# TensorE repeats a product of the identity in four places where it waits

## The chip, the cores and the metric

The kernel runs on one core of a Trainium2 chip. The core has a matrix engine (TensorE; its matmuls are PE in the profile, its weight loads PEld), a vector engine (VectorE, DVE), a scalar engine (ScalarE, ACT), GpSimd (POOL) and SyncE (SP), which issues most of the DMAs. Each engine works through its own instructions in the order in which the program gives them, and engines wait for one another through semaphores. The metric is the device time of one execution, in microseconds; lower is better.

## The reference

Sixteen images of 128 channels and 32 x 32 points, all in float32, pass through two layers. Each layer has two halves, and each half adds its result to its input:

```python
x = x + _L0_conv_ref(_ln_c(x), ...)      # attention, heads of 32, softmaxes over q and k
t = _to_tokens(x)
t = t + _L0_ffn_ref(_ln_t(t), ...)       # causal spectral filters (FFT convolution) and 3 taps
x = _from_tokens(t, x)
x = x + _L1_conv_ref(_ln_c(x), ...)      # conv 3x3, scale and shift, relu, conv 3x3, relu
t = _to_tokens(x)
t = t + _L1_ffn_ref(_ln_t(t), ...)       # 64 experts, each pools its 8 best tokens of an image
```

The last half in short: a gate gives each of the 1024 tokens of an image a logit for each of 64 experts; softmax over the tokens; each expert takes its eight largest, sums those tokens with the gate's weights, passes the sum through a hidden layer of 512 with a gelu, and adds its output back to the same tokens with the same weights.

## The kernel before

One program holds everything, with the queues' order fixed by hand or by a planner; the engines do not reorder it, and so a line of Python that stands earlier runs earlier on its engine. Lines are those of the profile of the kernel before.

The begin. `ident` (128 x 128) is built first. Sixteen samples of attention are laid out in the list `period`: each pass of the loop over `p` emits every name in the list once, for the sample `p + d`. Names that matter here are `tokens` (L152 transposes of an image into the PSUM tile `big`), `filters` (a generator that prepares the spectral filters; its first products are L644, from `wf` and `phi`), `group` (L390, the image's statistic), `norm` (L144 on ACT, eight slabs of 128 tokens), `channels` (L162 transposes back), `k` (L439) and `q_` (L421). A PSUM ring named `s` with two slots holds small tiles. Two small products (L338, `pw`, read by DVE's copies at L339) have used both slots before the first pass.

The spectral stage follows (L790 generates filters, L814 multiplies spectra with them, ACT copies each result `py` out at L875). Its last outputs are combined by DVE, written to DRAM and read back as `y` by layer 1.

Layer 1. A planner (`planned`) gives each step of `table` for each of the 16 samples a place in one order, from costs and due times. For the first image, TensorE starts with `inverse` (L1074: for the even classes it reads `y` itself, then POOL's `z`, and for the odd classes DVE's `z`, L1020). Then come `tokens` (L152), the convolutions in a transformed domain (L958 in `products`, PSUM ring `cv` with three slots of 128 x 512), `last` (DVE, L1219, the end of the convolution's half), and for every second image the steps of a pair of images: `logits` (L1261), `largest`, `exp`, `replace`, `gates`, `turn` (L152 on the gates, copied by ACT at L1301), `pool` (L1308), `pooled` (L1321). `channels` (L162) of the second norm feeds `logits` through ACT's copy `tk` (L1253). The order that the planner makes is kept by the loop over `order`.

The experts. Weights come as 32 transfers of 1 MB (`load_half`, `we`) into a ring of nine buffers, which are those that layer 1 uses up to then; transfer h + 9 waits until buffer h has been read. Groups of four experts run through `hidden` (L1482 on the weights and L1489 on the bias, both in four column groups of 32), gelu on ACT (L1494), `turn` (L1502), `output` (L1513) and `collect` (L1524). DVE then weights the outputs (`ob`, L1554) from transposes in `pob` (L1550), and the last sums (L1572, `pfy`) multiply gates and `ob`; DVE, or ACT and POOL, add them to `x` and the images are written.

The first transfers of gates and weights wait for `tk` and `tt` buffers of layer 1; `gates` of the last pair stay in SBUF.

```python
getattr(samples[b], arg[0])(*(
    getattr(samples[b], a) if a in ("va", "vb") else a for a in arg[1:]
))
```

Here the loop over `order` emits one step of one sample.

## Time and profile before

| | |
|---|---|
| median of three runs | 1273.64 us (1272.99 to 1274.5) |
| the profiled execution's own time | 1271.01 us |
| its span, first to last instruction | 1269.2 us |
| mean granted TensorE clock | 0.967 |
| PE busy | 1149.1 us, 91% of the span |
| weight loads | 934.4 us, 74% |
| DVE busy | 936.2 us, 74% |
| ACT busy | 725.9 us, 57% |
| POOL busy | 605.3 us, 48% |
| DMA | 164.64 MB, 130 GB/s over the span |

The stages, by the lines that run: attention to about 402 us, the spectral stage to 661, layer 1's convolutions and gates to about 1159, the experts to 1240, the last sums and the writes to the end.

A page of the profile divides the span into 40 slices and gives for each the busy share of each engine in tenths, the clock that was granted to TensorE (PEclk, tenths of full speed) and the share of the DMA engines that was busy. A line of a group shows the source line, engine, operation, written tile and read tiles, their shapes, how often, busy time and the mean of one. Matmul records are pipelined; a record's duration is longer than the distance to the next one, so a sum over many is read from the first start to the last end. A float32 matmul stands as two records where it is a product, and as one where it is a transpose. In the rows of one line, durations in ns are shortest/median/longest. The chain of waits follows the work that ended last back from the last instruction.

### The profile page before, as it was taken

Reading aid. Unit: us, or ns where it says so; the run is one execution under the profiler, and the core shown is the slowest. Engines: PE = TensorE matmul, PEld = TensorE weight load, DVE = VectorE, ACT = ScalarE, POOL = GpSimd, SP = SyncE. Lnnn points to the kernel's source line nnn. Section 1 sums busy time; section 2 is a strip of 40 time slices with the busy share of each in tenths; the row PEclk is TensorE's granted clock in tenths of the full one; section 3 lists DMA queues with packets and bytes.
Section 4 is the critical chain, followed back from the end, with each engine's and each line's share of the span. In section 5 each row is a group of like instructions: output and inputs, shape, how many; then the busy total and the mean of one; then the engine's idle time right before and its main releaser. Section 6 shows DMA issues by size and latency. Waiting matters only on the chain. (4 is left out here: it accounts for less than half of the span.)

```text
span 1269.2 us, 34025 instructions
## 1 busy us (share of the span) xinstructions
PE 1149.1 (91%) x14244; PEld 934.4 (74%) x14244; DVE 936.2 (74%) x1944; ACT 725.9 (57%) x1420; POOL 605.3 (48%) x801
## 2 busy tenths in 40 slices
PE   4889999999997999999976999999999999977975
PEld 3677777777776998888865888888898888853432
DVE  5788888888765777776765798889898888772325
ACT  4777777767654777777742354565565556542111
POOL 2335545565666688888863444333353442210002
PEclk9999999999998999999998999999999999985998
DMA  7105343443345244444458231213222212055976
GB/s 264 33 30 165 117 139 124 134 158 111 106 134 183 87 136 137 137 136 136 130 196 244 72 81 34 83 34 84 67 55 77 70 50 101 27 190 190 389 285 265
DMA packets 88346, 164.64 MB, mean 130 GB/s; under 512 B 5632, under 2 KB 41728, under 8 KB 87552
## 3 DMA queue, kind: packets, MB, share of 16 engines
q1 hardware_dynamic: 87312, 159.05, 38.6%
q0 software_dynamic: 880, 3.41, 0.8%
q8 instruction: 112, 1.84, 0.6%
q14 instruction: 42, 0.34, 0.1%
HBM read 105.03 MB, written 57.41 MB: 128 GB/s over the span
## 5 line engine op out<-in xcount | busy, mean ns | idle before, releaser
L958 PE MATMUL pcv<-v,cw 128*128 128x256 f32 x1152 | 259.7, 381 | 0.7 <-POOL v L1144 0.7
L958 PEld LDWEIGHTS pcv<-v,cw 128*128 128x128 f32 x1152 | 215.9, 191 | 34.3 <-issue 4.9
L801 DVE COPY g<-pg 128x512 f32<-128x512 f32 x196 | 127.8, 682 | 77.1 <-PE pg L790 77.1
L803 ACT COPY g<-pg 128x512 f32<-128x512 f32 x316 | 161.2, 605 | 31.7 <-PE pg L790 30.9
L790 PE MATMUL pg<-ph,mst 32*128 32x128 f32 x4096 | 139.6, 278 | 5.0 <-issue 3.5
L790 PEld LDWEIGHTS pg<-ph,mst 32*128 32x128 f32 x4096 | 126.0, 186 | 19.1 <-issue 12.4
L814 PE MATMUL py<-g,v 128*32 128x128 f32 x4096 | 127.9, 276 | 8.5 <-POOL v L781 5.7
L814 PEld LDWEIGHTS py<-g,v 128*32 128x32 f32 x4096 | 110.1, 111 | 18.3 <-POOL v L781 5.8
L144 ACT ACTIVATE tok<-tok,sts 128x128 f32<-128x128 f32 x256 | 101.9, 480 | 16.8 <-DVE sts L1031 13.4
L135 DVE BATCH_NORM_STATS2 bst<-big 128x6 f32<-128x256 f32 x256 | 91.1, 416 | 23.3 <-PE big L152 14.1
L781 POOL TENSOR_TENSOR v<-xc 128x256 f32<-128x256 f32 x128 | 99.8, 803 | 8.9 <-DMA xd<-x 8.9
L626 PE MATMUL big<-u,mu 128*128 128x128 f32 (+4 forms) x384 | 86.0, 380 | 0.0
L1144 POOL TENSOR_TENSOR v<-abss 128x256 f32<-128x256 f32 x64 | 49.1, 788 | 66.1 <-DVE abss L1140 54.3
L277 POOL TENSOR_TENSOR xf<-ab 128x256 f32<-128x256 f32 x34 | 24.8, 729 | 112.3 <-DVE ab L244 112.3
L1163 POOL TENSOR_TENSOR yo<-abss 128x256 f32<-128x256 f32 x32 | 23.5, 736 | 109.1 <-DVE abss L1159 109.1
L626 PEld LDWEIGHTS big<-u,mu 128*128 128x128 f32 x384 | 56.7, 191 | 18.0 <-issue 15.4
L875 ACT COPY yt<-py 128x512 f32<-128x512 f32 x64 | 37.5, 586 | 48.9 <-PE py L814 26.4
L1580 POOL TENSOR_TENSOR x<-yt,x 128x1024 f32<-128x1024 f32 x4 | 9.4, 2359 | 115.2 <-ACT yt L1579 115.2
L559 PE MATMUL big<-wf,ub 128*128 128x256 f32 x256 | 62.0, 385 | 0.2
L144 ACT ACTIVATE tt<-tt,sts 128x128 f32<-128x128 f32 x128 | 51.1, 481 | 14.6 <-DVE sts L1031 14.6
L152 PEld LDWEIGHTS big<-ident,x 128*128 128x128 f32 x384 | 46.0, 146 | 17.7 <-issue 10.5
L782 POOL TENSOR_SCALAR v<-v 128x256 f32<-128x256 f32 x64 | 55.2, 862 | 5.6
(247 smaller groups left out, 2480.5 us busy)
## 6 DMA issues: line engine op xcount, KB each, us to landing
we<-in_weight SPq DMA_DIRECT2D x32, 1024.0 KB, 9.9
vd<-xf SPq DMA_DIRECT2D x16, 1024.0 KB, 5.1
xc<-vd SPq DMA_DIRECT2D x64, 256.0 KB, 3.2
yd<-ys SPq DMA_DIRECT2D x32, 512.0 KB, 4.0
y<-yd SPq DMA_DIRECT2D x14, 896.0 KB, 6.7
x<-in_x SPq DMA_DIRECT2D x16, 512.0 KB, 4.6
mi<-in_M_phi SPq DMA_DIRECT2D x16, 512.0 KB, 4.7
xd<-x SPq DMA_DIRECT2D x16, 512.0 KB, 6.1
```

The lines of the kernel that those rows point to most:

```text
L135: nc.vector.bn_stats(bst[:, j : j + 2, :].rearrange("p j s -> p (j s)"), src[:, j : j + 2, :].rearrange("p j c -> p c j"),)
L144: nc.scalar.activation(dst[:, j, :], src[:, j, :], AF.Identity, bias=nm[:, j : j + 1], scale=r[:, j : j + 1],)
L559: nc.tensor.matmul(dst, self.ub[:, q, :], wf[:, q, :], start=True, stop=True)
L626: nc.tensor.matmul(self.pa[:, a:hi], mu[:, NF - 1 - si, tap, :], self.u[:, a - tap : hi - tap], start=(tap == 0), stop=(tap == KU - 1),)
L781: nc.gpsimd.tensor_tensor(vv[:, x, 1:, bs], e, o, op)
L782: nc.gpsimd.tensor_scalar(v[:, :, 0, bs], v[:, :, 2, bs], -1.0, None, ALU.mult)
L790: nc.tensor.matmul(pg[r][:, i], mst[rs, 4 * q + i, :], ph[rs, c, :], start=True, stop=True,)
L801: nc.vector.tensor_copy(dst, src)
L803: nc.scalar.copy(dst, src)
L814: nc.tensor.matmul(py[rows, x, kl, :], v[:, (x * NM + m) * JL + jl, 1 - ri : 3 - ri, :] .rearrange("p k b -> p (k b)"), g[:, ((x * 2 + ri) ...
L958: nc.tensor.matmul(pc[:, i], wt[:, dy, k, :], v[:, k, dy * WT : dy * WT + HT], start=(dy == 0), stop=(dy == 2),)
L1144: nc.gpsimd.tensor_tensor(v[:, k, WT : WT + HT], self.ab[:, 0], self.ab[:, 1], op)
```

## The change

A function `keep` takes a pool, a ring's name and a count. It takes one tile `wm` from that ring and writes the product of the identity with two copies of itself into it, `count` times over, 128 x 256 float32. Nothing reads the tile. Calls stand at these places of TensorE's order:

- the begin: nine after `tokens` of image 1, eight after the first products of the filters, three after `channels` of image 0, three after `k` of image 1;
- ahead of layer 1: thirty-three ahead of the first `inverse`;
- the last pair's chain: four after `turn` of images 12 and 13, eight after their `pooled`, eleven after `logits` of images 14 and 15, one after their `turn`;
- ahead of the last sums: four after the transposes into `pob`.

Together that is 84 products. The instructions of the other engines stay as they were and in the same order.

```diff
+    def keep(ps, tag, count):
+
+        if count:
+            wm = ps.tile([P, 2, P], F32, name="wm", tag=tag, bufs={"s": 2, "cv": 3}[tag])
+        for _ in range(count):
+            nc.tensor.matmul(
+                wm, ident, ident.unsqueeze(1).to_broadcast([P, 2, P]), start=True, stop=True
+            )
...
+            idle = {("tokens", 1): 9, ("filters", 0): 8, ("channels", 0): 3, ("k", 1): 3}
...
                         if name == "filters":
                             next(setting, None)
+                            keep(ps, "s", idle.pop((name, 0), 0) if p > -reach else 0)
                         elif 0 <= b < B:
                             if name == "tokens":
                                 samples[b] = Attention(b)
                             getattr(samples[b], "q_" if name == "q" else name)()
+                            keep(ps, "s", idle.get((name, b), 0))
...
+        idle = {(13, "turn"): 4, (13, "pooled"): 8, (15, "logits"): 11, (15, "turn"): 1}
...
             samples = [None] * B
+            keep(ps, "cv", 33)
             for b, name in order:
...
                     getattr(samples[b], a) if a in ("va", "vb") else a for a in arg[1:]
                 ))
+                keep(ps, "cv", idle.get((b, name), 0))
...
                     pob[:, q, :], ot[:, 2 * q : 2 * q + 2, :].rearrange("p j e -> p (j e)"), ident
                 )
+            keep(ps, "cv", 4)
             for q in range(NPAIR):
```

## The prediction

> **What bounds the kernel now.** I read the page's slices first: TensorE (PE) is busy in nine tenths of nearly every slice, so a stage gains if TensorE has less to do or does it faster. The row of the granted clock says where it is not at full speed.

> ```profile
> PE   4889999999997999999976999999999999977975
> ...
> PEclk9999999999998999999998999999999999985998
> DMA  7105343443345244444458231213222212055976
> ```

> Each slice is 31.7 us. The dips are at the end (slices 36, 37 and 40) and in the middle (26); the first slice hides another. What a clock level does to an instruction is in the rows of single lines: shortest, median and longest record of the pooling products and of the hidden layer's.

> ```profile
> L1308 PE MATMUL pp<-tt,gtt x256: 272/273/473, 809.3 to 1157.3; 128*64 128x128 f32 x128
> L1482 PE MATMUL ph<-we,pooled x128: 592/617/1063, 1159.1 to 1230.4; 128*32 128x512 f32 x128
> ```

> ```profile
> 657.58:660.99 3.41, 0.00 (x0) 0.00 (x0) 1.58 (x5) 1.52 (x3) 0.01 (x1) 1.00 0.90 311
> 660.99:664.40 3.41, 0.00 (x0) 0.00 (x0) 2.75 (x6) 0.00 (x0) 0.00 (x0) 0.50 1.02 360
> ...
> 1125.20:1128.62 3.42, 1.11 (x20) 1.11 (x22) 3.21 (x8) 3.32 (x8) 0.73 (x1) 1.00 0.98 286
> 1128.62:1132.03 3.41, 3.41 (x25) 2.82 (x22) 3.38 (x3) 0.77 (x3) 0.00 (x0) 0.50 1.04 389
> 1132.03:1135.44 3.41, 1.14 (x10) 0.90 (x9) 1.67 (x6) 1.85 (x2) 0.20 (x1) 1.00 0.99 336
> ...
> 1145.68:1149.10 3.42, 0.00 (x0) 0.00 (x0) 2.57 (x5) 0.69 (x1) 0.00 (x0) 1.00 0.81 252
> 1149.10:1152.51 3.41, 1.49 (x7) 1.52 (x8) 1.30 (x2) 0.51 (x2) 0.00 (x0) 0.50 0.84 320
> ```

> A stretch with 1.1 us of work or less is followed by half clock, a full one by full clock. Over the whole span, of the stretches at full clock, each that was 0.40 busy or less is followed by half clock, and none with 0.45 or more is. From 1149.1 the half clock lasts 23.9 us, to 1173.0, though PE is busy there; the chain of waits shows that this is where the end is made:

> ```profile
> 1140.68 4.79 PE big L1261 x8
> ...
> 1151.02 1.96 PE big L152 x8
> ...
> 1154.06 3.73 PE pp L1308 x32
> ...
> 1159.08 1.94 PE ph L1482 x8
> 1161.01 1.91 PE ph L1489 x8
> ...
> 1200.74 13.77 DMA we<-in_weight
> ...
> 1216.11 13.81 DMA we<-in_weight
> ...
> 1240.36 5.45 PE pfy L1572 x16
> ```

> So the last pair's logits, turn, pool and the first expert groups run at half speed on the chain; from 1200 the expert weights' stream sets the time.

> [...] The trace agrees: its half-clock spells are 1, 2, 3, 5 and 7 times 3.413 us. [...] here the stretch 26.11 to 29.52, nearly all transposes, was followed by full clock, so I count them. [...]

> **The change, part by part.** Nothing is removed. 84 products 128x256 are added, with PSUM tiles of existing rings and no DMA; other engines' orders stay. A conv product of that shape costs 0.454 us at full clock (24 records, 12 products, 5.45 us) and, at half, about 0.9 (estimate: doubled). PE runs in order, so a batch that outlasts its wait delays what follows. But for the batch ahead of layer 1 the ring slots cost no wait: their last readers end before (srow's copies at 9.6, shift's at 1120.5, sums at 1126.6, rows at 1128.5).

> *Begin (9, 8, 3, 3).* Until 19.3 the clock row reads 1.00, but the durations say half: 16 transposes at 7.26 took 3.68 us, 0.23 each, against 0.13 (1.04 for 8) at 35.23. The nine start at 10.95, partly at half clock, and end between 15.0 and 16.6, about when phi lands (15.97). The filters (L644, 5.31 us, three fifths at half clock) then take 8 x 0.454 = 3.6 us and end at about 20.0 instead of 21.3: -1.3, passed on by ACT, then DVE, to the first norm at 25.02. The eight (3.6 us, to 23.6) end before group's sum at 24.3. The next transposes fall from 1.77 to 1.0 us, and their statistics no longer stand ahead of the group's scale on DVE: -0.6. k, at 31.39, comes 1.9 earlier; I take -1.8. The threes fit the waits at 29.4 to 31.4 and 44.8 to 46.9. Bounds: -3.0; +0.9 if the clock rises only near 17.

> *Ahead of layer 1 (33).* The tile's bank makes the first product wait for the last copy of py (ACT L875, ending 660.91), so it starts at 660.95, after 3.37 us of idling that still drop the clock in most phases. At full clock the batch ends at 660.95 + 33 x 0.454 = 675.9, with one half-clock window (1.7 us lost) at 677.6, with two at about 679. Before, the first inverse started at 673.79. It is late, but its odd part waits for DVE's z at 678.04 anyway: batch end plus 1.9 us for the even part gives 677.8 (free), 679.5 or 681: +0, +1.4, +2.8. Behind it is the first sample's whole chain; the second conv product waits until 696.3 for an abss that DVE delays for y's DMA (landing 691.8), which absorbs some 0.7. I take +0.8, bounds 0 and +2.6.

> *Last pair's chain (4, 8, 11, 1).* The four (1.8 us) end at 1127.0, before pool at 1127.5; pool 2.67 becomes 1.97, the transposes 1.90 become 0.9, but the last sample's transposes wait for DVE's last (L1219, to 1131.83): -0.1 only. The eight run 1133.1 to 1136.7; norm's first slab comes at 1137.4. Channels stay paced by ACT's slabs: -0.2. Logits: copy of tk to 1141.4, then 1.86 us as at 1112.53 in the pair before, end 1143.3 instead of 1145.48: -2.2 in all. largest, replace, exp and gates take 5.54 us unchanged; the eleven (5.0 us) end at 1148.3, turn starts at 1148.85. Turn 1.96 to 1.0, pool 3.73 to 1.9 (1.97 for 32 at 1033.56), pooled -0.2: the first hidden at 1153.9 instead of 1159.08, -5.2. If the slab-paced stretch drops the clock (a grid stretch that mostly covers 1136.7 to 1140.3; about half of the phases), logits end some 1 us later: -0.5 on average.

> Then the groups stay at full clock: 7.4 us for a group become 3.9. But the stream decides. The last gates and the ninth weight wait for pool and for L1482, so the stream starts 5.2 earlier. From 1158 to 1174 DMA is busy 12.3 us of 16, 4.2 us under its later 1.05 share, because half-clock groups free buffers late; with 3.9 us groups I leave 1 us of these gaps. Stream end: -5.2 - 3.2 + 0.5 = -7.9. Bounds -10 and -4.

> *Last sums (4).* They follow the eight transposes (1238.03) and end at 1239.9; DVE's ob ends at 1240.32. The grid stretch 1237.84 to 1241.26 rises from 0.32 busy to 0.85, so pfy is not halved: its first pair ready at 1242.1 instead of 1243.33. After that DVE's sums (1.23 us each) and the 20 us of output writes follow: -1.3; bounds -2.0, 0.

> Sum: -1.8 + 0.8 - 7.9 - 1.3 = -10.2 us. On the profiled span, 1269.24 - 10.2 = 1259.0, and 1.8 lies around it: 1260.8. The timed runs' median is 2.6 above the profiled execution (1271.01); I take the sum from the median: 1273.64 - 10.2 = 1263.4, rounded to 1263.

> **Rivals.** *The stream does not follow*: the weights come no faster, only the first -5.2 of the tail passes, or clock drops recur: -1.8 + 0.8 - 4 - 1.3 gives 1267.3. For it: DMA is at 1.05 share from 1174 on. Against: its idle time ahead of that is seen. *More is gained*: the timed runs stand 2.6 above the profile, perhaps for more half-clock windows, which the change would take too, and the groups leave no gap: 1257. *Slower*: the products do not lift the clock, and cost 0.9 each. Place: ahead of layer 1, 33 x 0.9 = 29.7, inverse at 690.7, +16.9 and more than what is gained anywhere; the eleven add 4.4, in all about 1295. It decides from about 0.75 us a product (batch end 685.7, add some 9 to 10 late). Against: convs of that shape keep full clock for hundreds of us, and filters lifted it at 19.3. *No change*: it needs the worst bounds together, +2.6 ahead of layer 1, -4 for the stream and nothing at the begin and the last sums.

> **How the numbers follow.** Main 0.68, with 1259 to 1267; stream or drops 0.17 (1266 to 1271); more 0.09; no change 0.02; slower 0.04. A measurement tells 0.2%, 2.5 us. The range leaves out the slower case and the outer part of the others: 1256 to 1269. Faster 0.94, same 0.02, slower 0.04.

> **What would show it.** Right: full clock from 1125 to the end of the stream in nearly all windows; wm at 0.45 us; L1261's last record near 1143, L1308 of the last pair at 1.97, DMA above 1.0 from the ninth weight on. Wrong: the last yt copy does not hold wm; the first inverse after 679; pooled products ready but L1482 waiting for weights from the start; half clock again between 1140 and 1165, [...] (1159 to 1163 was full and did not lift the clock).

## The result, and the profile after

The changed kernel takes 1266.48 us in the median of 15 runs (1263.2 to 1273.87). The kernel before, timed beside it, takes 1276.9 us (15 runs). The ratio is 0.9918, interval 0.99 to 0.9936: 0.82% faster, or 10.4 us. The prediction had 1263 from 1273.64, which is 0.83%. The predicted ratio is right almost to the digit. The experiments below show that this is partly luck: the largest term is right by its mechanism, and the errors of the others cancel.

The profiled execution of the changed kernel is one of the slowest of the 15: 1273.16 us, span 1271.4. The kernel before had a span of 1269.2 in its profile, so the two profiles, laid side by side, show no gain at all. Each line below is to be read with this in mind; a second profile of both kernels follows further down. The page's slices of the changed kernel, busy tenths of TensorE, its granted clock and the DMA share:

```profile
PE   6889999999997999999998999999999999998976
PEclk9999999999998999999999999999999999999999
DMA  7005343443345344434348512223122211236986
```

The dips of the clock at slices 22, 36, 37 and 40 are gone. The one at slice 13 stays in both kernels: it is the begin of the spectral stage, with 6.8 us at half clock from 401.6 before and from 402.3 now, which the change leaves alone. The rows of the two lines that stood for half clock, the pooling products and the hidden layer's (shortest, median, longest record):

```profile
L1323 PE MATMUL pp<-tt,gtt x256: 272/273/324, 821.0 to 1165.0; 128*64 128x128 f32 x128
...
L1499 PE MATMUL ph<-we,pooled x128: 592/617/1059, 1166.5 to 1235.5; 128*32 128x512 f32 x128
```

No pooling product is at half speed any more (longest 324 ns, before 473). The hidden layer still has a record of 1059 ns. Where it is from, the table on the clock's grid of 3.41 us shows; columns as in the prediction:

```profile
665.14:668.55 3.41, 1.23 (x43) 0.96 (x33) 3.37 (x2) 0.00 (x0) 3.40 (x5) 1.00 0.94 326
668.55:671.97 3.42, 2.77 (x53) 2.77 (x56) 0.76 (x2) 0.58 (x1) 0.32 (x1) 0.50 0.94 260
...
675.38:678.79 3.41, 3.41 (x18) 3.00 (x17) 2.13 (x5) 0.00 (x0) 0.00 (x0) 1.00 0.59 234
...
1146.42:1149.84 3.42, 2.53 (x12) 1.78 (x10) 1.00 (x6) 2.25 (x6) 0.20 (x1) 1.00 1.01 365
...
1163.49:1166.90 3.41, 2.54 (x37) 1.86 (x39) 0.64 (x2) 1.47 (x5) 0.00 (x0) 1.00 0.09 17
1166.90:1170.31 3.41, 2.12 (x20) 0.62 (x12) 0.00 (x0) 2.86 (x6) 0.00 (x0) 1.00 0.95 363
1170.31:1173.73 3.42, 3.42 (x19) 0.49 (x17) 0.69 (x1) 0.00 (x0) 0.00 (x0) 0.50 0.62 238
1173.73:1177.14 3.41, 3.41 (x52) 1.68 (x52) 0.98 (x2) 0.60 (x1) 0.00 (x0) 1.00 0.89 309
```

Layer 1 is entered at full clock (675.38), and the last pair's chain runs at full clock. But one stretch in the first expert groups, 62% busy with the hidden layer's products, is followed by half clock. Two more things stand out: a stall of TensorE at 665 to 668, at the end of the spectral stage, and a DMA that stands nearly still from 1163.5 to 1166.9: the next weights are issued only at 1167.62, just after the group's first products on the weights (1166.49 to 1167.55). The chain of waits of the changed kernel:

```profile
1153.68 1.95 PE big L1276 x6
...
1161.17 1.08 PE big L152 x8
...
1163.33 2.02 PE pp L1323 x32
...
1170.71 1.86 PE ph L1499 x8
1172.57 1.57 PE ph L1506 x8
...
1205.65 13.77 DMA we<-in_weight
...
1221.02 13.94 DMA we<-in_weight
...
1244.86 3.75 PE pfy L1590 x16
```

The turn has fallen from 1.96 to 1.08 us, the pool from 3.73 to 2.02, the first `pfy` piece of the chain from 5.45 to 3.75. The weights' stream still ends the chain, as before. Yet the logits stand later than before in absolute time (1153.68 against 1140.68 for the piece): 12.1 us were lost ahead of DVE's last sum into `x` (1143.89 against 1131.83), in stages that the prediction called untouched or improved.

To find them, I cut every profile of this study at the same five events. Columns, in us: *begin*, from the start to the first spectral multiply (the first `py` product); *spectral*, from there to the end of the last copy of `py`; *layer 1*, to the end of DVE's last sum into `x`; *tail*, to the first transpose into `pob`; *first sum*, from there to DVE's first sum of a `pfy`; *end*, from that same transpose to the end. Median and ratio with its interval are of the timed runs, 6 to 22 for a row. Each ratio is against runs of the kernel before in the same batch, whose medians were 1276.9, 1276.35, 1275.18 and 1274.48, so two medians of the table do not make a ratio.

| kernel | begin | spectral | layer 1 | tail | first sum | end | span | median | ratio to before |
|---|---|---|---|---|---|---|---|---|---|
| before | 403.8 | 257.1 | 470.9 | 105.1 | 6.40 | 32.3 | 1269.2 | 1276.9 | |
| before, again | 404.6 | 254.9 | 470.6 | 105.0 | 6.78 | 32.9 | 1268.0 | 1271.6 | 0.997 (0.9951 to 0.9989) |
| changed | 403.8 | 270.9 | 469.2 | 98.1 | 4.90 | 29.4 | 1271.4 | 1266.5 | 0.9918 (0.99 to 0.9936) |
| changed, again | 403.5 | 264.3 | 471.2 | 96.5 | 4.90 | 29.4 | 1265.0 | 1264.4 | 0.9917 (0.9888 to 0.9945) |
| begin alone | 403.6 | 267.9 | 468.6 | 99.9 | 7.00 | 31.5 | 1271.5 | 1274.3 | 0.9988 (0.9968 to 1.0008) |
| 33 alone | 404.2 | 257.6 | 470.4 | 105.6 | 3.63 | 28.2 | 1266.1 | 1268.1 | 0.994 (0.9924 to 0.9955) |
| 33 alone, again | 405.6 | 257.0 | 470.9 | 106.0 | 3.64 | 28.2 | 1267.6 | 1266.6 | 0.995 (0.9934 to 0.9966) |
| last pair's 24 alone | 410.9 | 258.6 | 471.1 | 96.6 | 7.24 | 32.7 | 1269.9 | 1263.7 | 0.9919 (0.9888 to 0.9951) |
| last four alone | 407.9 | 257.7 | 470.8 | 105.0 | 5.44 | 30.0 | 1271.4 | 1272.1 | 0.997 (0.9951 to 0.9988) |
| changed without the 33 | 401.4 | 263.6 | 469.0 | 98.4 | 5.45 | 31.6 | 1264.0 | 1267.1 | 0.9944 (0.9926 to 0.9963) |
| changed without the begin | 411.7 | 259.0 | 470.6 | 97.9 | 4.90 | 30.1 | 1269.3 | 1264.1 | 0.992 (0.9892 to 0.9948) |
| begin, one column | 412.0 | 263.2 | 469.8 | 105.0 | 6.37 | 31.4 | 1281.5 | 1280.9 | 1.004 (1.002 to 1.0061) |
| changed, 256 instructions at the begin | 402.5 | 259.5 | 471.8 | 98.3 | 4.90 | 30.2 | 1262.3 | 1262.8 | 0.9911 (0.9878 to 0.9944) |
| same, 24 for 33, one more | 401.2 | 257.3 | 474.3 | 97.6 | 4.77 | 30.8 | 1261.2 | 1262.2 | 0.9907 (0.9876 to 0.9939) |

A row is one execution, so single entries carry the accident of that execution; groups of rows are what counts. The second row says how much a ratio can be trusted: the kernel before against itself gave 0.997, with an interval that leaves out 1. A ratio that is 0.3% away from another is therefore not taken as a difference here, whatever its interval says. The parts do not add up either: the four ratios of the parts alone (0.9988, 0.994, 0.9919, 0.997) multiply to 0.982, and the whole change has 0.9918. If each of them, and that of the whole, is divided by the 0.997 of the kernel before against itself, the product is 0.994 and the whole 0.995. The gain may thus be nearer 0.5% than 0.8%; one repeat of the kernel before does not settle it.

### The profile page after: what moved, and what is told of

It is laid out like the page before. It is cut to its first block, busy times and chain, and to the rows that moved or that the text cites. A ratio compares the mean times of both kernels' runs of the same rounds, so it can differ in the third digit from the quotient of the medians.

```text
span 1271.4 us, 34361 instructions
## 1 busy us (share of the span) xinstructions
PE 1174.9 (92%) x14412; PEld 959.3 (75%) x14412; DVE 940.1 (74%) x1944; ACT 725.5 (57%) x1420; POOL 604.1 (48%) x801
## 3 DMA queue, kind: packets, MB, share of 16 engines
q0 software_dynamic: 880, 3.41, 0.8%
q8 instruction: 113, 1.85, 0.6%
## 4 chain that ended last, share of the span: by engine, by line
PE 61%; DVE 21%; ACT 7%; DMA 5%; issue 4%; POOL 1%; SPq 0%; POOLq 0%; ACTq 0%; DVEq 0%
PE pcv L971 10%; PE pg L803 10%; PE py L827 10%; PE big L637 6%; DVE bst L135 4%; PE big L171 3%; PE big L152 3%; DMA we<-in_weight 3%; PE big L570 3%; PE big L450 2%; PE big L533 2%; PE big L432 2%; ACT tt L144 1%; DVE abss L1212 1%; PE wm L164 1%
## 5 line engine op out<-in xcount | busy, mean ns | idle before, releaser
L971 PEld LDWEIGHTS pcv<-v,cw 128*128 128x128 f32 x1152 | 215.5, 191 | 32.9 <-issue 4.9
L803 PE MATMUL pg<-ph,mst 32*128 32x128 f32 x4096 | 145.3, 281 | 13.4 <-issue 11.7
L803 PEld LDWEIGHTS pg<-ph,mst 32*128 32x128 f32 x4096 | 129.7, 187 | 30.2 <-issue 22.6
L135 DVE BATCH_NORM_STATS2 bst<-big 128x6 f32<-128x256 f32 x256 | 91.1, 416 | 22.2 <-PE big L152 12.9
L152 PEld LDWEIGHTS big<-ident,x 128*128 128x128 f32 x384 | 45.1, 143 | 19.1 <-issue 12.2
## 6 DMA issues: line engine op xcount, KB each, us to landing
we<-in_weight SPq DMA_DIRECT2D x32, 1024.0 KB, 10.1
```

The costliest lines, as they stand in the source:

```text
L135: nc.vector.bn_stats(bst[:, j : j + 2, :].rearrange("p j s -> p (j s)"), src[:, j : j + 2, :].rearrange("p j c -> p c j"),)
L152: nc.tensor.transpose(pt[:, j, :], src[:, j * P : (j + 1) * P], ident)
L803: nc.tensor.matmul(pg[r][:, i], mst[rs, 4 * q + i, :], ph[rs, c, :], start=True, stop=True,)
L971: nc.tensor.matmul(pc[:, i], wt[:, dy, k, :], v[:, k, dy * WT : dy * WT + HT], start=(dy == 0), stop=(dy == 2),)
```

## The experiments

### Each part alone

The four places were first tried one at a time, each time with `keep` and only the calls of one place.

```diff
+            idle = {("tokens", 1): 9, ("filters", 0): 8, ("channels", 0): 3, ("k", 1): 3}
...
+        idle = {}
```

> Only the 23 products at the begin. The prediction's step: 1.8 us faster than before (bounds 3.0 faster, 0.9 slower), k of the first image at 29.5 us instead of 31.4. Rival, after the changed kernel's profile, where phi landed at 16.3 us, the nine products had ended at 14.3, the clock fell again and k came at 31.1: the begin is worth 0.3 us.

Measured: 0.9988, not told from no change. The begin does what was expected of it: `k` starts at 29.45. But the spectral stage, whose instructions are those of before, takes 267.9 us instead of 257.1.

```diff
+            samples = [None] * B
+            keep(ps, "cv", 33)
             for b, name in order:
```

> Only the 33 products ahead of layer 1. The prediction's step: they end after the first image's spectra have landed and cost 0.8 us (bounds 0 and 2.6 slower). Rival: the clock stays up through the wait, the first inverse makes up for its late start, and the stage gains 1 us or more, counted from the last copy of the spectral stage to the first image's sum (19.2 us before).

Measured: 0.994. Layer 1 takes as long as before (470.4 against 470.9), and the first image's first inverse is done 19.2 us after the last copy of `py` in both, so the gain is not where the products stand. The table shows where it is: the first sum of `pfy` comes 3.63 us after the `pob` transposes and not 6.40, at the other end of the kernel. That is taken up below.

```diff
+        idle = {(13, "turn"): 4, (13, "pooled"): 8, (15, "logits"): 11, (15, "turn"): 1}
```

> Only the 24 products in the last pair's chain. The prediction's step: 7.9 us faster (bounds 4 and 10): first hidden product 5.2 us earlier, counted from the last image's sum, and the weights' stream ends 7.9 us earlier. Rival, the stream does not follow: 4 us faster, first hidden product as early but the stream's end no more than 5 us earlier.

Measured: 0.9919; the tail falls from 105.1 to 96.6 us. The spectral stage and layer 1 stay within 1.5 us; the begin is 7.1 us longer in this profile, which is taken up with the begin below. From the end of DVE's last sum to the first hidden product it is 22.6 us instead of 27.3, and from there to `pob` 74.0 instead of 77.9.

That the clock does this, and not something else that the products bring, is seen across all fourteen profiles. The tail follows its own time at half clock without exception: 96.5 to 97.6 us with none (three profiles), 97.9 and 98.1 with 3.4 us (two), 98.3 and 98.4 with 6.8 (two), 99.9 with 13.7, and 105.0 to 106.0 with 30.7 to 34.5 (six). The one with 13.7 is the begin alone, which has none of the 24 products and escaped the long spell; why, was not shown.

```diff
+            keep(ps, "cv", 4)
             for q in range(NPAIR):
```

> Only the four products ahead of the last sums. The prediction's step: 1.3 us faster (bounds 0 and 2.0), no half clock under the first sums, first sum on DVE 1.2 us earlier. Rival: the writes of the output set the end, and the time is the same within 0.3 us.

Measured: 0.997, which with the second row of the table is no proof by time. In its profile the first sum of `pfy` comes after 5.44 us, where the five profiles with neither these four nor the 33 have 6.4 to 7.2.

### The change without one part

```diff
-            keep(ps, "cv", 33)
```

> The change without the 33 products ahead of layer 1. The prediction's step (the 33 cost 0.8 us): about 11 us faster than before. Rival, after the run with the 33 alone (0.6% faster): the 33 earn most of what the whole change earns, and this kernel is only 2 to 5 us faster. Last copy of the spectral stage to the first convolution product: 32 to 33 us without the 33, 31 with them.

Measured: 0.9944. This is some 7 us faster than before, between the two values expected. Layer 1 is 469.0 us, the first sum 5.45: the values without the 33, and those of the four alone. The first convolution comes 29.5 us after the last copy, earlier than either value expected; in the mean it is 31.8 us without the 33 and 31.9 with them.

```diff
-            idle = {("tokens", 1): 9, ("filters", 0): 8, ("channels", 0): 3, ("k", 1): 3}
+            idle = {}
```

> The change without the 23 products at the begin. The prediction's step (the begin earns 1.8 us): about 8.5 us faster than before. Rival, after two profiles in which the spectral stage, first product of py to last copy, took 268 to 271 us with the begin's products and 257 to 259 in four without them: the begin's products lengthen that stage by some 10 us, which eats what they earn; this kernel is 14 us or more faster, and the stage takes 257 to 259 us.

Measured: 0.992, the changed kernel's ratio. That is some 10 us faster than before, between the two values expected. In the whole, then, the begin's 23 products bring nothing that the timing can tell. In the profile the loss and the gain are both plain: the first multiply comes at 411.7, and the spectral stage is 259.0. What the begin looks like without its products, in this kernel, on the grid:

```profile
22.36:25.77 3.41, 0.76 (x4) 0.33 (x2) 1.96 (x4) 1.00 (x3) 1.23 (x2) 1.00 0.03 13
25.77:29.19 3.42, 1.73 (x8) 1.73 (x9) 1.88 (x8) 2.36 (x7) 2.79 (x6) 0.50 0.00 0
29.19:32.60 3.41, 2.37 (x12) 1.97 (x10) 2.50 (x13) 2.31 (x7) 0.00 (x0) 0.50 0.78 211
32.60:36.01 3.41, 2.43 (x11) 2.43 (x12) 0.52 (x5) 3.38 (x9) 0.00 (x0) 0.50 0.41 154
36.01:39.43 3.42, 3.42 (x12) 2.39 (x11) 2.03 (x3) 1.43 (x5) 0.00 (x0) 0.50 0.00 0
39.43:42.84 3.41, 2.70 (x19) 1.93 (x17) 2.88 (x6) 2.22 (x3) 0.00 (x0) 1.00 0.03 5
```

One idle stretch is paid with four at half clock, 13.7 us: the next three, 0.51 to 0.71 busy, are followed by half clock again, and the fourth, wholly busy, by full clock. The changed kernel in the same time:

```profile
23.43:26.85 3.42, 2.43 (x15) 1.93 (x14) 2.71 (x10) 1.50 (x4) 3.42 (x7) 1.00 0.08 31
26.85:30.26 3.41, 3.26 (x19) 2.21 (x17) 2.57 (x13) 3.33 (x9) 0.24 (x1) 1.00 0.50 96
30.26:33.67 3.41, 2.59 (x20) 2.35 (x21) 1.04 (x6) 3.38 (x9) 0.00 (x0) 1.00 0.35 120
```

### The same instructions without their time

The begin alone, with products of one column per copy: the same 92 instructions, with little work in them. (In the changed kernel's profile its 84 products are 168 weight loads and 168 matmuls, two and two for each; for the begin's 23 that makes 46 and 46.)

```diff
-                wm, ident, ident.unsqueeze(1).to_broadcast([P, 2, P]), start=True, stop=True
+                wm[:, :, 0:1], ident, ident[:, 0:1].unsqueeze(1).to_broadcast([P, 2, 1]),
+                start=True, stop=True,
```

> Only the begin's 23 products, and of one column for each copy in place of 128, so that as many instructions are added but hardly any TensorE time. If the place of later instructions in TensorE's stream lengthens the spectral stage, it takes 266 us or more here too, and the kernel is some 10 us slower than before. If it is the clock or the earlier start, or chance, it takes 257 to 259 us and the time is as before within 2 us.

Measured: 1.004, slower than before. The clock stays at half at the begin for 13.7 us, from 25.67 to 39.32, so such products did not lift it here. The spectral stage is 263.2 us: longer than in any profile without the 92 instructions, though less than the 266 expected. This separates two things that go with the begin's products. With their full time, in the changed kernel, the clock is full from 20.02 to 402.31; with one column it was not. With their instructions, even when these take hardly any time, goes a longer stage 370 us later (263.2 us against 257.1). The groups of TensorE in the spectral stage, busy and idle time, of the kernel before and of the changed one:

```profile
L814 PE MATMUL py<-g,v 128*32 128x128 f32 x4096 | 127.9, 276 | 8.5 <-POOL v L781 5.7 <-POOL v L782 1.5 <-ACT g L803 0.8
L790 PE MATMUL pg<-ph,mst 32*128 32x128 f32 x3776 | 127.5, 277 | 3.6 <-issue 3.5
```

```profile
L803 PE MATMUL pg<-ph,mst 32*128 32x128 f32 x3776 | 133.2, 281 | 11.9 <-issue 11.7
L827 PE MATMUL py<-g,v 128*32 128x128 f32 x4096 | 128.9, 279 | 10.8 <-POOL v L794 6.4 <-issue 2.8 <-POOL v L795 1.0
```

The added idle time is "issue": TensorE waits for nothing that the profile shows. The three longest gaps ahead of `pg` (at 502.4, 537.6 and 554.6 us, 1.67, 1.21 and 1.07 long) each begin about 1 us after a packet of the DMA queue q8, whose kind is "instruction" in the profile (501.6, 536.4, 553.4). The kernel before has such gaps too, but all of TensorE's over 0.15 us make 6.0 us in this stage, against 16.1. The 10.1 us between them are the larger part of the 13.7 by which the stage grew.

This queue carries 112 packets with 1.84 MB in the kernel before, 16.4 KB each. Its packets go with TensorE's records: there are 112 again with the 92 of this run added, 113 with the changed kernel's 336 and 114 with the 500 of the run with 256 at the begin, below. Spread over the packets of the kernel before, its 14244 matmul and 14244 weight-load records are some 254 a packet (an estimate from these counts, as if the packets carried nothing else). In the five profiles with 92 instructions more ahead of it, the stage is 6 to 13 us longer than the mean of the nine others, 257.6.

The prediction counted transposes as work that lifts the clock, from one stretch, 26.11 to 29.52, which was 3.27 us busy and followed by full clock. Against it stands one of this run, 29.08 to 32.49, which transposes and one-column products filled wholly (3.41 us) and which half clock followed. Which of the two holds for transposes is not settled here.

### The changed kernel again

> The changed kernel once more. If the long spectral stage belongs to this program, it takes 268 to 272 us again; if it is chance, it may take 257 to 259 us, and the span is then near 1259. In either case 8 to 12 us faster than before.

Measured: 0.9917, the first ratio again, and a profile nearer the median: span 1265.0. The spectral stage is 264.3, neither of the two values expected, and still longer than in any profile without the 92. The clock did not fall in the expert groups, and the tail is 96.5 us.

### Moving the instructions by about one packet

By the estimate of 254 records a packet, 256 added instructions move those behind them by about one packet. The 92 move them by about a third of one.

```diff
+    def keep(ps, tag, count, w=P):
...
+                wm[:, :, 0:w], ident, ident[:, 0:w].unsqueeze(1).to_broadcast([P, 2, w]),
...
+            idle = {("tokens", 1): 22, ("filters", 0): 20, ("channels", 0): 11, ("k", 1): 11}
...
+                            keep(ps, "s", idle.pop((name, 0), 0) if p > -reach else 0, 46)
...
+                            keep(ps, "s", idle.get((name, b), 0), 46)
```

> The whole change, but the 23 products of the begin are cut into 64 narrower ones (128x92, 22, 20, 11 and 11 of them): 256 instructions instead of 92 stand ahead of the spectral stage[...] the stage from the first spectral multiply to the last yt copy is 257 to 259.5 us again, instead of 264.4 and 270.9 in the changed kernel, and the time is some 8 us under the changed kernel's, about 0.985 of the kernel before. Rival, that any added instructions or the higher clock ahead of it lengthen that stage: 263 us or more, and the changed kernel's time, 0.992. Begin: k at 29 to 31.5, first spectral multiply at 401 to 404.5.

Measured: the stage is 259.5 us, where the changed kernel's two profiles, and the one without the 33, have 263.6 to 270.9; the begin stays quick (402.5). The rival, that any added instructions or the higher clock lengthen it, falls for the stage. Over all profiles the sorting has no exception: nine with 0 or 256 more instructions ahead lie at 254.9 to 259.5, five with 92 more at 263.2 to 270.9. So does the "issue" time of TensorE ahead of `pg`: 1.7 to 5.2 us in the nine, 5.9 to 11.7 in the five. The time doesn't follow as expected. 0.9911 is only 0.0006 under the changed kernel's ratio, where 0.006 was forecast, and the interval (0.9878 to 0.9944) lies wholly above the forecast 0.985. In this profile, too, TensorE has 5.2 us of "issue" ahead of `pg` (3.5 before):

```profile
L804 PE MATMUL pg<-ph,mst 32*128 32x128 f32 x3776 | 128.5, 279 | 5.2 <-issue 5.2
L828 PE MATMUL py<-g,v 128*32 128x128 f32 x4092 | 127.3, 276 | 5.1 <-issue 2.0 <-DVE pooled L898 1.0 <-ACT g L817 1.0
```

So the stage's length goes with the number of instructions added ahead of it, 92 against 0 or 256. That their place within the packets is how, was my theory and is not shown, and what the shorter stage is worth in the median time is unsettled.

One more run takes this kernel, with its 256 instructions at the begin, and edits it in two more places: 24 products ahead of layer 1 in place of 33, and one after the first group's `hidden`.

```diff
+            keep(ps, "cv", 24)
...
                     hs[g] = hidden(g)
+                    keep(ps, "cv", g == 0)
```

> The kernel with the 64 narrower products at the begin, and two more edits: 24 products ahead of layer 1 instead of 33, and one more after the first expert group's hidden layer, in the wait for its gelu. If 33 outlast the wait by 9 x 0.454 = 4.1 us: from the last yt copy to the first convolution about 30 us instead of 32. If the first groups' windows are kept full: no clock drop between 1150 and 1175, first hidden to pob 74 us. Time 1 to 3 us under the kernel with the 64 narrower products alone. Rival, that the 33 are hidden by the wait for DVE's z: no difference.

Measured: 0.9907, not told from the run before it. With 24 products the first convolution comes 31.0 us after the last copy of `py` (32.0 with 33), but then an idle stretch at 692.7 is followed by 3.4 us of half clock, and layer 1 takes longer: 474.3 us. By an estimate from the hidden layer's eight records in the kernel before, 1.94 us at half clock and 1.00 at full, such a spell costs half its length, 1.7 us, so the rest of that is not explained. From 764.4 to the last sums no stretch is at half clock in this profile, and yet the tail, 97.6, is no shorter than without the one more product (96.5 to 98.4); the expected 74 us from the first hidden product to `pob` are 75.0.

### The 33, and the kernel before, once more

> The 33 products ahead of layer 1 alone, once more. By the stages of the first such run they are neutral (last yt copy to first convolution 32.0 against 32.0), and then the ratio is 0.998 to 1.002; if the first timing (0.994) was of this edit, it is 0.992 to 0.996 again. Where its profile has no half-clock spell of more than 3.4 us at 25 to 40 us, the begin is of the quick kind as before; the spectral stage, with the begin unchanged, is 257 to 259 us.

> The kernel before, once more, for a second profile of it. If its recorded begin was a lucky one, the half-clock spell at 25 to 40 us can be 10.2 or 13.7 us instead of 3.4 and the first spectral multiply then comes at 408 to 412 instead of 403.8; the spectral stage is 257 to 259 us in either case. Ratio 1.000 within 0.002.

Measured: 0.995 and 0.997, in one batch: 1266.57 against 1271.59 us, 5.0 apart. The kernel before missed the 1.000 that was expected of it. Against it and against the batch, the 33 gain 0.2 to 0.6%, with layer 1 unchanged for the second time (470.9 against 470.6). The lower of these is within what a repeat may differ by. What makes the gain credible is that both profiles have it, and at the same place: the end is 28.2 us in both, against 32.3 and 32.9. TensorE at the last sums in the kernel before:

```profile
1236.94 1.09 PE L1550 MATMUL big<-ident,ot 128*128 128x128 f32 x8 [0.36 <-DVE ot L1525]
1240.36 4.97 PE L1572 MATMUL pfy<-gt,ob 64*128 64x512 f32 x14 [2.33 <-DVE ob L1554]
```

With the 33 alone, second run:

```profile
1239.46 1.09 PE L1567 MATMUL big<-ident,ot 128*128 128x128 f32 x8 [0.36 <-DVE ot L1542]
1241.08 4.22 PE L1589 MATMUL pfy<-gt,ob 64*128 64x512 f32 x17 [0.52 <-DVE ob L1571]
```

And in the changed kernel:

```profile
1241.97 1.09 PE L1567 MATMUL big<-ident,ot 128*128 128x128 f32 x8 [0.36 <-DVE ot L1542]
1242.91 1.89 PE L164 MATMUL wm<-ident 128*128 128x256 f32 x8
1244.86 4.55 PE L1590 MATMUL pfy<-gt,ob 64*128 64x512 f32 x18
```

Before, the first `pfy` waits 2.33 us for DVE, to the end of all eight slices of `ob`. With the 33 it waits 0.52 us, for the first slice. The cause is in the PSUM banks that the built program gives its tiles. Before, `pob` lies in the bank pair (from bank 0 on) that the first `pfy` takes over, and so the first `pfy` waits until DVE has read all of `pob`. The tile `wm` of the 33 is the first of layer 1's pool, so the ring `cv` now gets the first banks and `big`, with `pob` in it, begins at bank 3; the third `pfy`, needed later, is the first to wait for `pob`. The programs with the 33, or with 24 in their place, have `big` there, and those without have it at 0. No run took the tile without its products, so that the bank is the cause rests on this allocation and on the two waits.

The start of `pfy`, 1.8 us earlier, is one part of what the first sum gains (3.63 against a mean of 6.75). The other, 1.3 us, is the clock, which falls under the first sums in all five profiles with neither the 33 nor the four (from 1241.26 to 1244.67 in the kernel before) and in neither with the 33 alone. It is the same 1.3 us that the four alone gain, which leave the start of `pfy` at 3.42. With the 33 there is no half clock left for the four to prevent. In the changed kernel the four last products stand in the gap that the new banks would open: they end 2.82 us after the first `pob` transpose, and `pfy` starts at 2.89 where it started at 1.62 with the 33 alone, so there the four only cost.

## Why the prediction was right, and where not

**Total.** Predicted -10.2, measured -10.4 in the first comparison and the same ratio in the second. By the stage table the parts are not those of the sum. The term of the last pair is right, in size and in mechanism. That the total agrees so closely is luck: a begin that is worth more than forecast, a spectral stage that was forecast at nothing and lost time, and an end that gains by a bank that was not thought of.

**Begin (-1.8, bounds -3.0 and +0.9): the size was wrong.** `k` came 2.6 us earlier in the mean (29.8 over six profiles with the products against 32.4 over eight without), which is within the bounds. But the term stopped at `k`. What the idle stretches cost goes on behind it, and the profile of before that I read was of the mildest kind. Over the eight profiles without real work there, the spell of half clock that begins between 23.9 and 27 us is 3.4 us (before, 33 alone), 6.8 (before again, 33 again), 10.2 (the four alone) or 13.7 (three), and the first spectral multiply comes at 403.8 and 404.2, 404.6 and 405.6, 407.9, and 410.9 to 412.0, in the same order. With the products it comes at 401.2 to 403.8. The mean is 402.6 against 407.6: -4.9. The step on the filters failed in detail: in the changed kernel's profile the nine ended at 14.26, `phi` landed only at 16.26, and the filters were as slow as before (5.38 us).

**The missing term: the spectral stage.** The prediction said that nothing moves but TensorE's added products, and gave the stage between none. It grew by 13.7 us in the changed kernel's first profile and by 7.2 in its second. By the profiles this more than cancels the begin's gain, and the change without the begin is as fast (0.992). By the time it isn't settled: the kernel with 256 instructions keeps the early begin and the short stage, and is faster by 0.0006 only.

**Layer 1 (+0.8, bounds 0 and +2.6): right by the stage.** The six profiles with the 33 have 469.2 to 471.8, mean 470.7; the seven without have 468.6 to 471.1, mean 470.1: +0.6. The first inverse starts later (14.4 us after the last copy of `py` with the 33 alone, 12.9 before) and is run at full clock, and both are done after 19.2 us. The step had counted on the wait for `z` to absorb the delay, not on the clock. What the step left out is that a tile in an existing ring can move the ring. "With PSUM tiles of existing rings" was taken to mean that nothing else changes; it moved `pob` away from `pfy`.

**Last pair's chain and stream (-7.9, bounds -10 and -4): right.** The tail is 96.5 to 98.4, mean 97.6, in the seven profiles with the 24 and 105.0 to 106.0, mean 105.3, in six of the seven without; the seventh, the begin alone, has 99.9, with less half clock than the six. That is -7.7. The first half was -5.2 at the first hidden product and measured -4.7 (27.25 against 22.60 in the changed kernel); the logits' share, -2.2, measured -1.9. The sign that I named for the second half failed: the DMA is not above 1.0 from the ninth weight on, and stood at 0.09 from 1163.5 to 1166.9, since the next weights were issued only at 1167.62. The stream followed nevertheless, by another 2.4 us in the first profile and 3.9 in the second, whose expert groups had no half clock.

**Last sums (-1.3, bounds -2.0 and 0): right alone.** The four alone bring the first sum from a mean of 6.75 to 5.44 us. In the changed kernel it is 4.90, of which the 33 have the larger part: with them alone it is 3.63. There the four cost 1.3 us by their own time. The change without the four was not tried.

**The clock's bound.** "At most 0.40 is followed by half clock, and none with 0.45 or more" fell: in the changed kernel a stretch 0.62 busy (1166.90, above), with the bias products that use 64 of the 128 rows, was followed by half clock. The changed kernel's second profile has a stretch with just as much, which full clock followed, so that the busy share alone does not decide:

```profile
1163.26:1166.67 3.41, 2.12 (x20) 0.74 (x16) 0.69 (x1) 1.65 (x2) 0.00 (x0) 1.00 1.03 380
1166.67:1170.08 3.41, 3.41 (x56) 1.66 (x52) 0.93 (x2) 0.60 (x1) 0.00 (x0) 1.00 0.82 262
```

The other half of the rule, a full stretch followed by full clock, did not hold in the kernel before itself. These two were wholly busy, and half clock followed each:

```profile
1138.86:1142.27 3.41, 3.41 (x8) 1.31 (x9) 0.00 (x0) 2.31 (x5) 0.00 (x0) 0.50 0.18 74
...
1159.34:1162.75 3.41, 3.41 (x16) 0.20 (x8) 0.00 (x0) 2.26 (x5) 0.00 (x0) 0.50 0.90 309
```

The prediction had named the second as a danger; the hidden layer's products on the weights and on the bias (L1482 and L1489, from 1159.08 and 1160.94) run in it. In the first there are the transposes of L162 and the logits. Why the clock stayed at half after these was not shown. The dip that the prediction reads at slice 26 is not in its row, which has it at 13 and 22.

**The timed runs.** By the means, begin -4.9, spectral +6.7 to +13.2 (the two profiles of the change against 257.6, the mean of the nine), layer 1 +0.6, tail -7.7, and end -2.4 (the four profiles with both the 33 and the four unaltered, 29.8, against 32.2) make -7.7 at best. Measured is -10.4. About 3 us are not found in the stages, and two profiles can't find them, since this stage alone differed by 6.5 us between them.

## What to carry to other kernels

Filling TensorE's waits pays where the end waits for what it then does at half speed: here the last pair's 24 products, timed alone, give the ratio of the whole change (0.9919 and 0.9918). Before pricing such a wait, take several profiles of the same kernel, for here the half clock behind one idle stretch at the begin was 3.4 us in one profile of the kernel before and 6.8 in the other, and 13.7 in three programs with no real work added there. A tile that nothing reads is still a tile and its products are still instructions: look at which bank it pushes whom into, and at the stages behind it for new idle time that waits for nothing.

## What the runs showed of the hardware that I had not expected

- Ninety-two more TensorE instructions ahead of a stage that they don't touch went with 6 to 13 us more in it, even when they took hardly any time (263.2 against 257.1 us); 256 more did not (259.5 and 257.3).
- At half clock, a stretch wholly busy with transposes and one-column products (29.08 to 32.49, in the run with one column), and others 0.71 and 0.73 busy with attention's products, were followed by half clock again; one stretch with 0.76 us of work was so followed by four of half clock, 13.7 us.
- Two stretches of one program at full clock, each with 2.12 us of TensorE work in 20 records at the first expert groups, were followed by half clock in one profile (1166.90) and by full clock in the other (1163.26).
- The same program, run again beside itself, gave 0.997 with an interval of 0.9951 to 0.9989.
